# Shared experts woven into the two ends of a state-space layer whose mixing becomes one pipeline over 16 tiles

## The chip, the core and the metric

The kernel runs on one core of one Trainium2 chip. A core has five engines that run at the same time, each through a queue of its own and in the order of that queue: PE (TensorE, matmuls and transposes), DVE (VectorE), ACT (ScalarE), POOL (GpSimd) and SP (SyncE, which here only issues transfers). They meet through semaphores. Transfers between the off-chip memory and the on-chip memory (SBUF) run on 16 DMA engines. Matmul results go to eight banks of accumulation memory (PSUM). The metric is device time in microseconds (us) for one execution, and the time before is the median of three runs.

## The reference, cut to what matters

Input `x` has 8 sequences of 256 tokens, 256 wide, all fp32. Four layers follow one another, each with a residual and a layer norm (no learned scale):

```python
x = _layernorm(x + _L0_attn_ref(x, ...))   # 16 heads of 128, causal
x = _layernorm(x + _L0_ffn_ref(x, ...))    # mixture: 32 experts of width 96, top 6
x = _layernorm(x + _L1_attn_ref(x, ...))   # state-space layer
x = _layernorm(x + _L1_ffn_ref(x, ...))    # mixture: 16 experts of width 176, top 4
```

The first mixture scores the 32 experts by a sigmoid, keeps six a token with weights normed to sum 1, and adds a shared expert of width 192 that every token takes. The second scores 16 experts by a softmax, keeps the best two of four groups of experts, then the best four experts in them, and has a shared expert of width 352. An expert is `(silu(x Wg) * (x Wu)) Wd`.

The state-space layer, for each sequence:

```python
gate, hBC, dt = split(x @ in_proj_w.T)              # 512, 640, 8
h, Bm, Cm = split(silu(causal_conv4(hBC) + conv_b)) # 512, 64, 64
dt = softplus(dt + dt_bias);  A_d = -exp(A_log) * dt
L  = exp(segment_sum(A_d))                          # decay from token s to token l
y  = ((Cm @ Bm.T) * L) @ (h * dt) + carried state + D * h    # 8 heads of 64
yf = y * silu(gate)
return (norm_w * yf * rsqrt(mean(yf * yf) + 1e-6)) @ out_proj_w.T
```

The reference cuts a sequence into chunks of 32 and carries a state between them. The kernel uses chunks of 128, which gives the same sums.

## The kernel before, in words

**Tokens.** The 2048 tokens are four groups (`NG`) of 512, and a group is four tiles (`GT`) of 128. `x` stays in SBUF (`xg[g]`) through all layers.

**Order of the work.** The program is written with generators: a part of the work is a Python generator that yields between steps, and `weave` takes steps from several in turn, each at its own rate. `extras` holds generators from which `extra()` takes a step inside another loop. The result is a program order. A scheduler then orders the instructions of each engine from it by dependences and its own estimates, so an instruction can stand well ahead of its place in the text. At run time each engine takes its own list strictly in order, and a waiting instruction holds up all behind it.

**Mixtures.** `route` (L258 on) makes the choice of experts for one group: turns `x` (L267, L270), logits (L275), top weights (`combine0` or `combine1`), and a row number in the expert's bucket for each choice. For each of the group's four tiles it then fills a buffer `xe` with one row per choice: `x` (L328, ACT), the row's destination (L332, DVE) and its weight (L335, DVE). POOL sends the rows to the buckets in off-chip memory by indirect DMA (L337, one for each choice and tile: 24 a group in the first mixture, 16 in the second). `xe` and the gathered results `gy` share one pool of four buffers (`rowpool`, tag "r").

`sure_tiles` and `other_tiles` make a table of tiles of 128 rows with an expert each: 127 in the first mixture (41 of them known before the last group is routed), 79 in the second (33). `routed` (L530 on) walks the table: load the rows (L558, SP), transpose (L462), gate and up products (L473), SiLU (L478), product (L480), transpose (L489, L491), down product (L500), scale by the weight (L584), and an indirect DMA of the results (L585, POOL). `results` (L599) gathers a token's rows again, `combined` (L622 on) adds them to `x`, and `normed` (L606 on) is the layer norm; its `pow` runs on POOL (L617).

`shared` (L506 on) does one group of the shared expert and calls `extra()` between its steps. `mixture` (L900 on) loads the experts' weights in four parts (two DMAs each, from `load_weights`, L436 on), does `early` groups of the shared expert, the routed tiles, and then `late`. In the first mixture `early` is 3 and the fourth group follows the routed tiles. In the second it is 2 and the other two follow.

**State-space layer.** For each group, `combined` first finishes the first mixture (`all_combined`). `front(g)` then turns `x` (L1034), makes the time steps (`time_steps`, L991 to L1022), the decays `e` for each tile and half of the heads (ACT writes `r` for eight heads, L1067; PE sums, L1071; ACT takes the exp, L956), the convolution (`convolved`: product `cv` L971, first tap on ACT L977, three more on DVE L980), `gm` = C by B (L1099, L1103) and the gates `gt` (L1123). `back(g)` is a pipeline of slots over the group's four tiles: slot s starts tile s (h by dt L1147, `e` by `gm` L1157, state L1165), does y of tile s-1 (L1188, L1196, L1200 to L1209, mean square L1214 to L1216 with a `pow` on POOL), turns tile s-2 (L1225, L1227), and does the output product and norm of tile s-3 (L1235, L1239). So a group has 4 + 3 slots, and the next group's begin after them. `curve` keeps ACT's exps together and its SiLUs together, since they use different tables.

While `back(g)` runs, `weave` mixes in `front(g+1)`, `all_combined(g+2)` and the second mixture's `route(g-1)`; `route(3)` runs beside the second mixture's shared expert and routed tiles. The second mixture's expert weights lie in memory that the state-space layer used, so their load starts when that layer's last step is done.

## Time and profile before

| | us |
|---|---|
| median of three runs (1575.38 to 1586.15) | 1578.88 |
| the profiled execution | 1570.75 |
| its span on the core | 1569.0 |
| PE busy | 1441.7 (92%) |
| DVE busy | 850.4 (54%) |
| ACT busy | 613.9 (39%) |
| POOL busy | 415.8 (27%) |

| stretch of the span, us | what is in it |
|---|---|
| 0 to 688.8 | attention, with the first mixture's routing of groups 0 to 2 |
| 688.8 to 744.7 | start of the first mixture: route(3), shared experts, first rows |
| 744.7 to 930.8 | its 127 routed tiles |
| 930.8 to 1010 | last shared group, the first results gathered, the first front |
| 1010 to 1247 | state-space mixing, up to its last output product |
| 1247 to 1311.1 | start of the second mixture: two shared groups, weights loaded |
| 1311.1 to 1510 | its 79 routed tiles |
| 1510 to 1569 | two shared groups, results, last norms and output |

Durations come from one profiled execution. A line of the profile names the source line, the engine, the operation, what it writes and reads, and how often. "Idle before" is time in which the engine stood before such an instruction, and the name after the arrow is what came last of the things it waited for.

### The profile page before, as it was taken

How to read it: one execution, taken by the hardware profiler on the slowest of the kernel's cores; microseconds unless marked ns; L12 is line 12 of the kernel's file. 1: busy time of each engine (PE TensorE's matmuls, PEld its weight loads, DVE VectorE, ACT ScalarE, POOL GpSimd, SP SyncE). 2: the span in 40 equal slices, each digit the busy share in tenths (PEclk: the TensorE clock that was granted, in tenths of full speed). 3: DMA queues.
4: the chain of work that ended last, by engine and by line, in shares of the span. 5: the costliest groups of instructions: out<-in, count | busy, mean ns of one | idle time of the engine just before them, and what ended most of it. 6: DMA issues, size and time to landing. Idle time of an engine off the chain costs nothing. (4 is left out here: it accounts for less than half of the span.)

```text
span 1569.0 us, 22431 instructions
## 1 busy us (share of the span) xinstructions
PE 1441.7 (92%) x6643; PEld 1025.4 (65%) x6643; DVE 850.4 (54%) x3142; ACT 613.9 (39%) x1620; POOL 415.8 (27%) x474
## 2 busy tenths in 40 slices
PE   8999999999999999987999992899898779999996
PEld 5666666666667666665988881367474647777764
DVE  3444565446445644555655657747565535444457
ACT  3333433334333423341444542675656321333322
POOL 1000014000500032005566661001414315334332
PEclk9999999999999999998999995999999979999998
DMA  9999999900200011058455527100101282332335
GB/s 363 414 413 413 413 408 374 312 4 1 82 1 0 1 44 37 1 166 246 133 181 155 171 85 273 64 1 1 55 1 55 72 251 78 108 106 89 97 116 168
DMA packets 83477, 233.44 MB, mean 149 GB/s; under 512 B 12498, under 2 KB 47345, under 8 KB 81471
## 3 DMA queue, kind: packets, MB, share of 16 engines
q1 hardware_dynamic: 65727, 189.81, 34.7%
q0 software_dynamic: 17632, 42.20, 7.6%
q8 instruction: 56, 0.92, 0.3%
q14 instruction: 62, 0.51, 0.1%
HBM read 80.21 MB, written 157.76 MB: 152 GB/s over the span
## 5 line engine op out<-in xcount | busy, mean ns | idle before, releaser
L769 PE MATMUL qkp<-xT,wattn 128*128 128x512 f32 x512 | 242.0, 594 | 0.0
L804 ACT ACTIVATE pr<-neg,least 128x128 f32<-128x128 f32 (+1 forms) x256 | 114.4, 448 | 296.7 <-DVE least L799 296.6
L337 POOL DMA_INDIRECT m0xs<-m0xe,m0rows x96 | 92.9, 968 | 211.7 <-issue 128.3
L585 POOL DMA_INDIRECT m0ys<-m0ys,m0xl x127 | 125.0, 984 | 67.0 <-ACT m0ys L584 55.8
L777 DVE COPY qk<-qkp 128x512 f32<-128x512 f32 x64 | 44.2, 691 | 171.9 <-PE qkp L769 171.9
L769 PEld LDWEIGHTS qkp<-xT,wattn 128*128 128x128 f32 x512 | 91.1, 191 | 70.0 <-issue 68.5
L754 PE MATMUL vp<-wattn,xT 128*128 128x512 f32 x256 | 117.4, 596 | 4.6 <-ACT xT L218 3.1
L229 POOL TENSOR_TENSOR rstd<-rstd,root 128x1 f32<-128x1 f32 x16 | 8.8, 552 | 424.4 <-DVE rstd L228 422.7
L835 PE MATMUL op<-wattn,z 128*128 128x256 f32 x512 | 120.5, 382 | 0.0
L799 DVE CUSTOM_DVE_ANT_0 neg<-sc,cmask 128x128 f32<-128x128 f32 (+1 forms) x256 | 81.5, 355 | 58.0 <-PE sc L789 57.1
L585 POOL DMA_INDIRECT m1ys<-m1ys,m1xl x79 | 77.7, 984 | 111.4 <-ACT m1ys L584 104.4
L835 PEld LDWEIGHTS op<-wattn,z 128*128 128x128 f32 x512 | 92.6, 190 | 15.0 <-ACT z L857 4.8
L822 PE MATMUL zp<-pT,v 128*128 128x256 f32 x256 | 77.5, 384 | 5.0 <-DVE pT L820 4.9
L337 POOL DMA_INDIRECT m1xs<-m1xe,m1rows x64 | 62.8, 981 | 68.5 <-ACT m1s_1s L478 39.9
L754 PEld LDWEIGHTS vp<-wattn,xT 128*128 128x128 f32 x256 | 46.7, 191 | 48.4 <-issue 40.7
L789 PE MATMUL sc<-qk,qk 128*128 128x256 f32 x256 | 76.5, 380 | 0.0
L810 DVE TENSOR_SCALAR pr<-pr,total 128x128 f32<-128x128 f32 (+1 forms) x256 | 70.1, 318 | 3.3
L822 PEld LDWEIGHTS zp<-pT,v 128*128 128x128 f32 x256 | 47.7, 191 | 36.0 <-ACT z L857 11.8
L617 POOL TENSOR_TENSOR rstd<-rstd,root 128x1 f32<-128x1 f32 x48 | 32.9, 687 | 143.5 <-DVE rstd L616 132.2
L816 PEld LDWEIGHTS pt<-ident,pr 128*128 128x128 f32 x384 | 47.4, 142 | 32.4 <-issue 29.5
L820 DVE COPY pT<-pt 128x384 f32<-128x384 f32 x128 | 67.0, 550 | 2.9 <-PE pt L816 2.1
L785 PEld LDWEIGHTS sc<-qk,qk 128*128 128x128 f32 x256 | 43.7, 190 | 22.7 <-issue 20.4
(2974 smaller groups left out, 3148.6 us busy)
## 6 DMA issues: line engine op xcount, KB each, us to landing
m0xs<-blank SPq DMA_DIRECT2D x9, 7740.0 KB
m1xs<-blank SPq DMA_DIRECT2D x4, 7740.0 KB
m0xl<-m0xs SPq DMA_DIRECT2D x127, 129.0 KB
m0gy<-m0ys SPq DMA_DIRECT2D x16, 768.0 KB
m1xl<-m1xs SPq DMA_DIRECT2D x79, 129.0 KB
m1gy<-m1ys SPq DMA_DIRECT2D x16, 512.0 KB
wattn<-in_w_heads SPq DMA_DIRECT2D x16, 384.0 KB
m0w<-in_w_gu SPq DMA_DIRECT2D x4, 1536.0 KB
```

Source lines behind the costliest of these rows:

```text
L337: ins = nc.gpsimd.indirect_dma_start(out=d["xs"], out_offset=bass.IndirectOffsetOnAxis(ap=rows[:, k, t : t + 1], axis=0), in_=xe[:, k, :], ...
L585: ins = nc.gpsimd.indirect_dma_start(out=d["ys"], out_offset=bass.IndirectOffsetOnAxis(ap=row[:, DM : DM + 1].bitcast(I32), axis=0), in_=y ...
L754: nc.tensor.matmul(ps, lhsT=xT[:, k, t * P : (t + 1) * P], rhs=w_vq[q][:, k, :], start=(k == 0), stop=(k == KC - 1),)
L769: nc.tensor.matmul(ps, lhsT=w_head[h][:, at : at + P], rhs=xT[:, k, :], start=(k == 0), stop=(k == KC - 1),)
L789: nc.tensor.matmul(sc[:, P:], lhsT=qT[:, c0 + P : c0 + SEQ], rhs=kT[:, c0 : c0 + SEQ], start=True, stop=True,)
L799: nc.vector.tensor_tensor_reduce(out=neg[:, cols], in0=sc[:, cols], in1=cmask[:, cols], scale=-SCALE, scalar=3.0e38, op0=ALU.add, op1=ALU.min,
L804: nc.scalar.activation(pr[:, cols], neg[:, cols], AF.Exp, bias=least[:, i : i + 1], scale=-1.0, accum_out=total[:, i : i + 1],)
L810: nc.vector.tensor_scalar_mul(pr[:, cols], pr[:, cols], total[:, i : i + 1])
L816: nc.tensor.transpose(pt[:, i * P : (i + 1) * P], pr[:, i * P : (i + 1) * P], ident)
L820: nc.vector.tensor_copy(pT, pt)
L822: nc.tensor.matmul(zps[:, b * SEQ : (b + 1) * SEQ], lhsT=vs[2 * b][:, cols], rhs=pT[:, : 2 * P], start=True, stop=False,)
L835: nc.tensor.matmul(ps[:, :DM], lhsT=zs[i][:, t * P : (t + 1) * P], rhs=w_head[q * QH + i][:, 4 * P :], start=(i == 0), stop=(i == QH - 1),)
```

## The change

The arithmetic is the same apart from where one product is made. What moves, and where to:

- `shared` becomes a generator, so that it can be woven. In the first mixture only group 0 is done ahead of the routed tiles. Groups 1 and 2 follow after `all_combined(0)`, and group 3 is woven with `front(0)` and `all_combined(1)`. In the second mixture group 0 is woven into the last slots of the state-space layer, group 1 stands ahead of the routed tiles, and groups 2 and 3 follow them as before. The woven ones use a pool of their own (`shsb`, three buffers).
- The expert weights come in eight parts (16 DMAs) for four (8 DMAs). The second shared expert's weights are loaded after the first group's front.
- `back` runs over all 16 tiles as one pipeline of 16 + 3 slots. `front(g+1)` has slots 4g to 4g+4, `all_combined(g+2)` 4g to 4g+3, and `route(g)` 4g+8 to 4g+11, while group g's own tiles start in slots 4g to 4g+3.
- `front` is split into `turned_group`, `decays` (time steps and `e`) and `inner` (convolution, `gm`, gates). For group 0 `inner` comes first.
- `r` for heads 4 to 7 is one DVE product of 128x512 for each tile, in place of four ACT copies of 128x128.
- `e` has 10 buffers for 12, `gt` 7 for 8. The exp in `combine1` is kept with the other exps while the state-space layer runs.

```diff
@@ shared
-                extra()
+                yield
@@ mixture
-            w = load_weights(m, gu, dn, wpool, 0, m.n, 4, f"{m.name}w")
-            for g in range(early):
-                ex.shared(g, wsh)
+            w = load_weights(m, gu, dn, wpool, 0, m.n, 8, f"{m.name}w")
+            for _ in ex.shared(early, wsh):
+                extra()
@@ after0 and the first mixture
-        for g in range(NG - 1, NG):
-            ex.shared(g, wsh0)
-    mixture(M0, w_gu0, w_dn0, wsh0, NG - 1, after0)
-    wsh1 = load_weights(M1, w_gu1, w_dn1, wshared, E1, E1 + 2, 1, "m1ws")
+    mixture(M0, w_gu0, w_dn0, wsh0, 0, after0)
@@ weave
+        for n, gen, start, end in parts:
+            step = (Fraction(end) - Fraction(start)) / (n + 1)
+            live.append([Fraction(start) + step, step, gen])
@@ decays
-                    for i in range(HB):
-                        h = q * HB + i
-                        nc.scalar.activation(
-                            r[:, i, :], tri[:, :P], AF.Copy, scale=a[:, t, h : h + 1]
+                    if q:
+                        nc.vector.tensor_mul(
+                            r, tri[:, :P].unsqueeze(1).broadcast_to([P, HB, P]),
+                            a[:, t, q * HB :].unsqueeze(2).broadcast_to([P, HB, P]),
                         )
+                    else:
+                        for i in range(HB):
+                            nc.scalar.activation(
+                                r[:, i, :], tri[:, :P], AF.Copy, scale=a[:, t, i : i + 1]
+                            )
...
-                    e = act.tile([P, HB, P], F32, name=f"e{g}_{t}_{q}", tag="e", bufs=12)
+                    e = act.tile([P, HB, P], F32, name=f"e{g}_{t}_{q}", tag="e", bufs=10)
@@ front
+            yield from turned_group(g)
+            if g == 0:
+                yield from inner(g)
+                yield from decays(g)
+            else:
+                yield from decays(g)
+                yield from inner(g)
@@ back
-        def back(g):
-            for s in range(GT + 3):
-                t = s
-                if t < GT:
+        def back(lo, hi):
+            for s in range(lo, hi):
+                if s < NG * GT:
+                    g, t = divmod(s, GT)
@@ the order
-        take((COMBINE, all_combined(0)))
-        take((FRONT, front(0)), (COMBINE, all_combined(1)))
-        for g in range(NG):
-            parts = [(BACK, back(g))]
-            if g + 1 < NG:
-                parts.append((FRONT, front(g + 1)))
-            if g + 2 < NG:
-                parts.append((COMBINE, all_combined(g + 2)))
-            if g > 0:
-                parts.append((ROUTE, route(M1, g - 1, w_gate1, combine1)))
-            take(*parts)
+        weave((COMBINE, all_combined(0), 0, 1))
+        for g in (1, 2):
+            weave((SHARED, sh0.shared(g, wsh0), 0, 1))
+        weave(
+            (FRONT, front(0), 0, 1), (COMBINE, all_combined(1), 0, 1),
+            (SHARED, sh0.shared(3, wsh0), 0, 1),
+        )
+        wsh1 = load_weights(M1, w_gu1, w_dn1, wshared, E1, E1 + 2, 1, "m1ws")
+        parts = [(9, back(s, s + 1), s, s + 1) for s in range(NG * GT + 3)]
+        for g in range(NG - 1):
+            at = g * GT
+            parts.append((FRONT, front(g + 1), at, at + GT))
             if g + 2 < NG:
+                parts.append((COMBINE, all_combined(g + 2), at, at + GT - 1))
+            parts.append((ROUTE, routed_group(g), at + 2 * GT, at + 3 * GT - 1))
+        parts.append((SHARED, sh1.shared(0, wsh1), NG * GT, NG * GT + 3))
+        weave(*parts)
@@ after1 and the second mixture
-        ex.shared(NG - 2, wsh1, lambda: finish(2))
-        ex.shared(NG - 1, wsh1, lambda: finish(1))
+        for g, n in ((NG - 2, 2), (NG - 1, 1)):
+            for _ in ex.shared(g, wsh1, lambda: finish(n)):
+                pass
-    mixture(M1, w_gu1, w_dn1, wsh1, NG - 2, after1)
+    mixture(M1, w_gu1, w_dn1, wsh1, 1, after1)
```

## The prediction

> **What bounds the kernel now.** I read the stages first: the span was cut where PE's work changes hands, and each stretch was set against its granted clock and its DMA share. Attention (0 to 688.8 us) is not touched. In this view the first two columns are the stretch and its length, and each engine has its busy us and its instructions.
>
> ```profile
> core 0: us, PE busy (x) PEld busy (x) DVE busy (x) ACT busy (x) POOL busy (x), PEclk, DMA share, GB/s
> 688.80:744.70 55.90, 39.46 (x200) 33.38 (x199) 31.91 (x141) 16.32 (x38) 23.46 (x26) 0.88 0.88 265
> 744.70:930.80 186.10, 183.51 (x1146) 164.68 (x1147) 110.56 (x381) 91.13 (x252) 120.67 (x123) 0.99 0.51 151
> 942.90:1012.00 69.10, 34.62 (x92) 17.54 (x93) 51.58 (x146) 30.79 (x67) 6.90 (x10) 0.68 0.51 183
> 1010.00:1247.00 237.00, 217.55 (x1050) 148.38 (x1049) 142.95 (x527) 136.18 (x299) 57.48 (x70) 0.94 0.06 21
> 1247.00:1264.40 17.40, 5.43 (x8) 2.35 (x8) 4.62 (x29) 4.70 (x8) 13.82 (x17) 0.62 0.96 315
> 1264.40:1311.10 46.70, 42.45 (x182) 30.63 (x183) 21.60 (x107) 12.04 (x27) 5.73 (x6) 0.89 0.52 157
> 1311.10:1510.00 198.90, 197.70 (x954) 146.46 (x953) 88.99 (x258) 62.08 (x157) 85.02 (x88) 1.00 0.31 94
> ```
>
> The reader should see that PE fills both routed stages (744.7 and 1311.1 onward) and most of the state-space stage (1010 to 1247), so PE work added there costs its full time. PE is half idle at four seams: the start of the first mixture, the first front (942.9 to 1012, where DVE is the busy engine and the clock is 0.68), two stalls inside 1010 to 1247, and the tail 1247 to 1311. The change moves PE work between these. Next I read the instructions in time order at each seam; the brackets give the idle time before a row and what ended it.
>
> ```profile
> 731.76 0.48 PE L462 MATMUL m00xp<-ident,m0xl 128*128 128x128 f32 x1 [5.87 <-DMA m0xl<-m0xs]
> ...
> 1119.96 0.17 DVE L332 COPY m1xe<-m1dest 128x4 int32<-128x4 int32 x1 [4.52 <-DMA m1xs<-m1xe,m1rows]
> ...
> 1124.06 3.75 PE L971 MATMUL cv<-xT,win 128*128 128x512 f32 x4 [6.63 <-DVE conv L980]
> 1194.93 3.75 PE L971 MATMUL cv<-xT,win 128*128 128x512 f32 x4 [6.14 <-DVE conv L980]
> ...
> 1246.91 0.33 SPq L444 DMA_DIRECT2D m1w<-in_w_gu  x1
> 1251.05 2.72 PE L473 MATMUL m1s_0gu<-m1ws,m1xT 128*128 128x352 f32 x4 [4.20 <-DVE x L1239]
> 1260.69 2.71 PE L473 MATMUL m1s_1gu<-m1ws,m1xT 128*128 128x352 f32 x4 [6.92 <-DVE x L1239]
> 1313.08 1.42 PE L473 MATMUL m10gu<-m1w,m10xT 128*128 x4 [1.20 <-DVE m11xT L466]
> ```
>
> The first row is the earliest routed tile reaching PE. The next three are one chain: the four `xe` buffers are free only when the scatters that read them have landed, the DVE copy into such a buffer (L332) stands at the head of DVE's queue, the convolution step behind it (L980) is late, and PE's `cv` matmul starves. The last four are the tail: the second mixture's weights are asked for at 1246.9, when the last `out` ends.
>
> **The change, part by part.** Times are against the profiled execution: 1570.75 us, of which the span is 1569.0. The median of the runs shown is 1578.88, so 8.1 us (0.5%) are added at the end.
>
> *Start of the first mixture.* Groups 1 and 2 of its shared expert leave PE. A tile of it is two gate/up sets of 0.65 us (705.28 to 705.93), two transposes of 0.11 and two down sets of 0.43: 2.4 us, 9.5 a group. But 19 us are not won. The weights (4 x 1536 + 4 x 768 KB, issued 689.1 to 694.2) keep the DMA share at 1.01 from 690 to 726, and the first `m0xl` row set, queued behind them, lands for 731.76. Today PE still has shared work up to 744.7; afterwards it waits idle, and the first routed gate/up can follow the transposes and copies by about 4 us: 735.7 for 744.7. **-9** (0 if the tile table or scatters are later than the rows; -12 if the rows come 3 us sooner without the other traffic). POOL has 24 scatters of 0.96 + 0.30 us up to 745.5, and the first result scatters now queue into them; POOL needs 1.28 us a tile to PE's 1.47 (186.1/127), so it catches up.
>
> Eight parts for four means 8 more DMA issues. Row: the eight issues now take 0.33 to 1.7 us each on SP and the engines stay full, so parts overlap and cost 0. The Trainium skill (DMA: Bandwidth & Descriptors, "Anatomy of one DMA") speaks against small parts: each DMA has about 2 us that don't shrink with its size; put end to end that would be +16. The full DMA share decides for 0, and the first row set waits for all parts anyway, so no gain either.
>
> *First front.* Those two groups return here: 19 us of PE at full clock, perhaps 26 at 0.68, inside 34 us of idle PE: hidden. On DVE they aren't: products 2 x 0.24, copies 2 x 0.28, one add 0.42, so 1.5 us a tile and 11.7 for two groups; the r operation adds 4 x 0.68. That makes 51.6 + 11.7 + 2.7 = 66 of 69.1 us. About 5 of this can go into the 12 us in which DVE waits for the first gathered rows (930.8 to 942.9), and before there were 17 us of stalls, of which some 10 remain. Convolution ahead of the time steps for group 0 lets PE start `cv` earlier, but then the decays come last. I take **+2**, with -8 (the order hides all stalls) and +8 (no DVE work goes into the wait) as bounds.
>
> *r by DVE.* 64 ACT copies leave (0.39 us mean, 25 us of ACT) and 16 DVE products of 128x512 come. Nearest row:
>
> ```profile
> L1157 DVE TENSOR_TENSOR e<-e,gm 128x512 f32<-128x512 f32 x32 | 21.2, 677 | 0.0
> L337 POOL DMA_INDIRECT m1xs<-m1xe,m1rows x57 | 56.0, 983 | 66.4 <-ACT m1s_1s L478 39.9 <-issue 12.2 <-DVE m1xe L335 8.2
> ```
>
> So 16 x 0.68 = 11 us of DVE, hidden while DVE is at 60% in the steady stage; were it on the path, +11. ACT's relief is worth at most the 7 us that PE waits for `r`. Here too the skill warns (SBUF — State Buffer, "SBUF: two separate sides"): a DVE operation with two SBUF inputs shuts out a GpSimd operation that reads SBUF for its whole length. By the rule 16 scatters could each wait 0.68, 11 us of POOL. The rows show scatters at 0.983 us in this stage, with many such products beside them, and 0.968 in the first mixture: 15 ns each. I take **0**.
>
> *Steady pipeline.* No boundary is left between `back` calls, but PE is at 29.6 of 30 and 49.0 of 50 us in the stretches between the stalls, so I give that 0. The second mixture's shared expert of group 0 enters slots 16 to 19: per tile two gate/up sets of 1.19, two of transposes 0.22, two down sets 0.87, so 4.55 and 18.2 a group. About 13 of it stands ahead of the last `out` in the changed order, where PE has 2.8 us idle of 47: **+13** (+9 if it fills these and the wait for the last mean square, +16 if DVE's part, 8 us, delays the chain). `e` with 10 buffers for 12 and `gt` with 7 for 8 cost 0 while DVE runs ahead; exp kept beside the other exps saves table loads of 1.28 us on ACT, which is under 60% busy.
>
> The stalls now: PE lost 12.8 us in them (the 6.63 and 6.14 of the two `cv` rows). In the changed order the `xe` copies stand early again, because there are still four buffers and a group's scatters still take 16 x 1.27 = 20 us: group 1's copies wait for group 0's scatters between the convolution steps of the last front, and group 2's wait for group 1's between the gating products (`yf`) of the last `back` tiles. The first place costs PE about 8 us, as each of today's does at 6 to 7; the second about 13, because `rms` and `rstd` on POOL also queue behind the scatters there and no front is left for PE to do meanwhile. That is 20 to 21 for 12.8: **+7** (-5 if the copies pass in time; +27 if DVE stands through both drains, 40.6 us).
>
> *Tail.* From last `out` (1246.9) to `m10gu` (1313.1) are 66.2 us. Two shared groups are done in it, one is left (18.2). In the changed order POOL has the last `rms` ahead of route(2)'s scatters, so the waits of 4.20 and 6.92 shrink. What then ends last is the weights: 8 parts, 8.65 MB, asked for at the last `out`. DMA is at 0.96 till 1264 and falls after about 1280; with the row tiles behind them the floor is near +41. DVE's copies for group 2 and one shared group bring me to +46: **-20** (-25 at the floor, -10 if DVE is held by a whole drain).
>
> Both routed stages and the end (1510 to 1569) keep their instructions: 0.
>
> Sum: -9 + 2 + 0 + 13 + 7 - 20 = **-7 us**: 1563.8 for 1570.75, and 1572 for the median of 1578.9, which is 0.4% less.
>
> **Rivals.**
>
> *Faster, 1548.* A group's route has its slots later, when less of a front is left to hold up: stalls -5 for +7, shared work fills the last drain (+9), the tail reaches its weights (-25), start -10, front 0: -31. For it: 12.8 us of stall and 92 us of idle PE at the seams are there to be filled. Against: the `xe` buffers aren't changed, and they are what stalls.
>
> *Slower, 1602.* DVE's queue stands behind L332 through the whole of each group's scatters: +27 in the steady stage, and in the tail the third drain holds `x` and the shared hidden states (-10 for -20): -9 + 2 + 13 + 27 - 10 = +23. For it: DVE already waits up to 4.8 us in one such copy, and the change adds DVE work ahead of them. It decides once PE loses more than 27 us behind L332 in the steady stage (12.8 + 7 + 7); below that the sum is not above zero. Against: the order puts some `conv` steps and products between one copy and the next.
>
> *The start doesn't move, 1581.* Should the weights, then rows, table and scatters end when the shared work ended, the -9 is gone, and the rest sums to +2.
>
> **How the numbers follow.** Likeliest case 0.42 (its own range 1562 to 1588), faster 0.31, slower 0.21, no start 0.06. One per cent, 16 us, is about what a measurement of this kernel can tell from no change. The likeliest and the no-start case lie within it but for small ends: same 0.43; faster over 1% 0.32; slower over 1% 0.25. The range 1546 to 1601 leaves out a tenth on each side: the faster case's better half-tail, and a stall beyond both drains.
>
> **What would show it.** Start: PE idle from about 712 to 732 and the first `m00gu` near 736. Front: the first `e` by `gm` product near 1003 (1012 less 9), DVE over 85% busy in it. Steady: PE idle of 20 us behind DVE at two places, with L332 behind scatters in DVE's waits. Tail: first `m1w` issue to `m10gu` 46 us. I am wrong if these two places vanish, if the waits at L332 pass 40 us before the last `out`, or if the first front grows beyond 80 us because the shared work runs ahead of the gathers it hides.

## The result, and the profile after

The changed kernel takes 1599.87 us (median of four runs, 1598.53 to 1602.71) for 1582.04 before (1575.38 to 1586.15): a ratio of 1.0119, 95% interval 1.0076 to 1.0162. It is 1.2% slower, where 0.4% less was forecast. The profiled execution took 1601.04 us with a span of 1599.3, against 1570.75 and 1569.0, so the two traces differ by 30.3 us of span. The medians differ by 17.8 only: the profiled execution of the kernel before was 11.3 us faster than this median, so the table adds up to more than the change cost, and which row holds the surplus can't be told. Each stage runs from one event to the next; the marks are read from the two timelines. The first weight issue itself comes 0.7 us later, which with the differences below makes the 30.3 but for rounding.

| from, to | before, us | after, us | difference | forecast |
|---|---|---|---|---|
| first weight issue to first routed gate/up | 55.7 | 41.7 | -14.0 | -9 |
| to the last routed y, and the first gathered rows | 198.2 | 216.8 | +18.6 | 0 |
| to the first `e` by `gm` product (front) | 67.3 | 74.6 | +7.3 | +2 |
| to the end of the last `out` (steady, first part) | 236.7 | 261.2 | +24.5 | +20 |
| to the first issue of the second mixture's weights (steady, the rest) | 0.1 | 14.1 | +14.0 | 0 |
| to the first gate/up of the second mixture (tail) | 66.2 | 42.5 | -23.7 | -20 |
| to the end | 255.9 | 258.7 | +2.8 | 0 |

The view of busy time by stretch, of the changed kernel, with the columns as before:

```profile
689.70:731.40 41.70, 21.07 (x88) 16.88 (x87) 19.42 (x81) 11.95 (x21) 2.77 (x4) 0.66 0.95 273
731.40:760.00 28.60, 18.05 (x87) 15.95 (x87) 10.12 (x39) 4.77 (x15) 21.59 (x24) 0.74 0.37 124
760.00:935.90 175.90, 170.26 (x1059) 152.17 (x1060) 102.41 (x360) 85.66 (x237) 119.92 (x122) 0.99 0.54 158
948.30:1022.90 74.60, 52.23 (x205) 36.31 (x205) 60.05 (x188) 25.44 (x56) 9.30 (x12) 0.80 0.43 152
1022.90:1284.10 261.20, 236.91 (x1111) 160.33 (x1110) 156.43 (x557) 132.67 (x275) 53.59 (x69) 0.91 0.06 22
1284.10:1298.10 14.00, 7.16 (x25) 5.43 (x24) 2.86 (x11) 2.97 (x6) 10.86 (x12) 0.73 0.29 104
1298.10:1340.60 42.50, 27.05 (x117) 19.40 (x116) 18.81 (x107) 8.59 (x17) 3.22 (x4) 0.78 0.89 256
```

The first routed tiles start early and then stall: from 731.4 to 760 PE works only 18 of 28.6 us, while POOL is busy for 21.6. Up to the last `out` there are 19.4 us more of PE work than before, and 24.3 us of PE idle for 19.5. Then comes a stretch of 14 us that the kernel before does not have. In the tail the DMA share is 0.89, for 0.63 before.

Where the early start went is read from the timeline of the changed kernel (POOL, then ACT and PE):

```profile
729.43 1.02 POOL L337 DMA_INDIRECT m0xs<-m0xe,m0rows  x1 [35.92 <-DMA m0xl<-m0xs]
...
752.26 1.00 POOL L585 DMA_INDIRECT m0ys<-m0ys,m0xl  x1 [0.30 <-issue]
...
754.77 0.47 ACT L584 ACTIVATE m0ys<-m04y,m0xl 128x256 f32<-128x256 f32 x1 [9.69 <-DMA m0ys<-m0ys,m0xl]
...
755.30 1.22 PE L500 MATMUL m05y<-m0w,m05hT 96*128 x2 [8.97 <-ACT m0ys L584]
761.68 1.22 PE L500 MATMUL m06y<-m0w,m06hT 96*128 x2 [3.24 <-ACT m0ys L584]
```

The last group's 24 row scatters begin at 729.43, where before they began at 715.33. They waited for a row load (`m0xl`). The first result scatter stands behind 18 of them, at 752.26. There are four `ys` buffers, so tile 4's result waits for a buffer on ACT, and PE stands 9.0 and 3.2 us. Tile 1's `y` is 13.0 us earlier than before, tile 7's 3.1 us later, and from tile 26 on all are 4.9 to 5.0 us later.

What PE waited for from 1022.9 us to the first issue of the second mixture's weights (us in total, times, longest):

```profile
PE m1s_1hp L489 <- DVE m1xe L332: 6.8, 1, 6.8
PE out L1265 <- DVE hd L1176: 5.7, 2, 5.2
PE m1s_1gu L473 <- DVE m1s_0h L480: 4.8, 1, 4.8
PE m1xTp L267 <- ACT x L620: 3.4, 1, 3.4
```

The two `cv` waits of 12.8 us are gone, and these have come. The 14 us are read from the timeline (PE and SP), and from what SP waited for at the first of these issues, in the changed kernel and in the kernel before:

```profile
1250.68 2.72 PE L473 MATMUL m1s_1gu<-m1ws,m1xT 128*128 128x352 f32 x4 [4.85 <-DVE m1s_0h L480]
...
1275.70 1.35 PE L473 MATMUL m1s_0gu<-m1ws,m1xT 128*128 128x352 f32 x4
...
1282.16 1.89 PE L1265 MATMUL out<-wout,yfT 128*128 128x256 f32 x8
...
1294.03 0.63 PE L489 MATMUL m1s_1hp<-ident,m1s_1h 128*88 128x128 f32 x2 [6.84 <-DVE m1xe L332]
...
1296.15 1.91 PE L500 MATMUL m1s_y<-m1ws,m1s_1hT 88*128 88x256 f32 x4
...
1298.13 0.36 SPq L444 DMA_DIRECT2D m1w<-in_w_gu  x1
```

```profile
SPq L444 <- PE m1s_y L500: 264.8, 1, 264.8
```

```profile
SPq L444 <- PE out L1235: 257.2, 1, 257.2
```

The last `out` ends at 1284.05. The second mixture's weights are not asked for then, but at 1298.13, when PE has ended the last down product of the woven shared group. In the kernel before, the same issue waits for the last `out` and follows it by 0.07 us. The reason is read from the kernel: the woven group's pool (`shsb`) is opened together with the state-space layer's pools, and the weights take the memory of that layer when its last step is done, so the group has become one of its steps. Half of the 14 us is one wait of 6.8 us, for a product on DVE that stands behind two others: a copy at L332 that waits 3.5 us for row scatters, and a norm that waits 4.2 us for its power step on POOL, itself behind row scatters.

All eight kernels here with this group in the drain (the last slots of the pipeline) ask for the weights 0.07 us after its last down product, 6.6 to 14.1 us after the last `out`. In the others it is 0.07 us after the last `out`, in one 0.57. No run moved the pool to other memory, so what the 14 us would be worth is not measured.

### The profile page after: what moved, and what is told of

Its sections match the earlier page's. It is cut to its first block, busy times and chain, and to the rows that moved or that the text cites. A ratio compares the mean times of both kernels' runs of the same rounds, so it can differ in the third digit from the quotient of the medians.

```text
span 1599.3 us, 22358 instructions
## 1 busy us (share of the span) xinstructions
PE 1457.3 (91%) x6643; PEld 1037.6 (65%) x6643; DVE 859.8 (54%) x3158; ACT 594.2 (37%) x1556; POOL 414.4 (26%) x474
```

## The experiments

The runs fell on two kinds of chips: on one the kernel before takes 1576 to 1582 us (medians), on the other about 1680, chiefly in attention and the first mixture. Why is left open. So totals are compared as ratios to the kernel before on the same chip, and stages only between chips of one kind. Below, "steady" runs from the first `e` by `gm` product to the first issue of the second mixture's weights, and "tail" from there to the first gate/up. The recorded expectations call that first mark the last `out`, which holds only where the group is out of the drain. "Both back" is the changed kernel with both shared experts where they were.

### The first mixture's shared expert

One part undone: groups 0 to 2 ahead of the routed tiles, group 3 behind them.

```diff
-            for _ in ex.shared(early, wsh):
-                extra()
+            for g in early:                  # first mixture (0, 1, 2), second (1,)
+                for _ in ex.shared(g, wsh):
+                    extra()
...
     def after0(ex):
+        for _ in ex.shared(NG - 1, wsh0):
+            extra()
...
-        for g in (1, 2):
-            weave((SHARED, sh0.shared(g, wsh0), 0, 1))
         weave(
             (FRONT, front(0), 0, 1), (COMBINE, all_combined(1), 0, 1),
-            (SHARED, sh0.shared(3, wsh0), 0, 1),
         )
```

> The changed kernel with the first mixture's shared expert put back where it was: groups 0 to 2 ahead of the routed tiles, group 3 behind them, the rest as changed. Theory (POOL gives the early start back, and the front pays on DVE): the first routed gate/up returns to about 745 us, the last routed y to about 931, the first e by gm product comes 67 us after the first gathered rows instead of 75, so about 12 us less than the changed kernel, near 1588 us. Rival (the early start is worth its 9 to 13 us and the loss lies in the later stages alone): 0 to 9 us more than the changed kernel, 1600 to 1609.

Measured: 1576.38 us, ratio 0.9985 (0.9953 to 1.0017), by the ratios 1.3% (some 21 us) less than the changed kernel and no different from before. The rival falls. The stages, by the same view:

```profile
942.10:1004.30 62.20, 33.39 (x96) 16.97 (x97) 52.34 (x153) 22.57 (x42) 8.81 (x12) 0.70 0.56 203
1004.30:1274.80 270.50, 239.02 (x1123) 162.95 (x1122) 158.39 (x565) 134.88 (x279) 64.82 (x81) 0.91 0.06 22
1274.80:1317.20 42.40, 27.30 (x117) 19.58 (x116) 18.86 (x107) 8.60 (x17) 3.23 (x4) 0.78 0.88 260
```

The first gate/up goes back to 743.89 and the last routed `y` to 929.68, 5.7 us earlier than in the changed kernel. The front takes 62.2 us for 74.6, with 7.7 us less of DVE work. So the three moved groups cost 12.4 us in the front, and the rest of the change makes the front 5.1 us shorter than before. The steady stage is 4.8 us shorter; in the changed kernel some of the last moved group's products had spilled into it.

### The late row scatters

The last group's routing is stepped to its end before the routed tiles are written down; nothing else changes.

```diff
             if m is M0:
                 load_mixer()
+                while len(extras) > 1:
+                    extra()
             ex.routed(w)
```

> The changed kernel with the last group's routing stepped to its end ahead of the first mixture's routed tiles, so that its 24 row scatters no longer wait for the row loads of the first tiles. Theory (POOL's late scatters hold the result scatters): POOL starts them at about 719 instead of 729 us and ends them by 749.5, the y of tile 7 comes at about 755 instead of 765, 9 to 11 us less than the changed kernel, near 1590. Rival (the result scatters are slow for another reason, such as the weights' traffic): no change, 1597 to 1602.

Measured: 1587.52 us, ratio 1.0065 (1.0042 to 1.0089), by the ratios 0.5% (some 8.5 us) less than the changed kernel. The two intervals overlap a little, but the spans of the traces differ by as much, 9.0 us. The timeline:

```profile
720.20 1.02 POOL L337 DMA_INDIRECT m0xs<-m0xe,m0rows  x1 [27.38 <-issue]
...
750.62 1.00 POOL L585 DMA_INDIRECT m0ys<-m0ys,m0xl  x1 [0.30 <-issue]
...
757.11 1.08 PE L500 MATMUL m07y<-m0w,m07hT 96*128 x2
```

The scatters start at 720.2 for 729.4, and tile 7's `y` comes at 757.1 for 764.9: the theory holds. This shows the first half of the loss: `shared` takes an `extra()` step between its own steps, and the routing of the last group lives on those steps. With one group of `shared` for three, there are 10 steps for 30. The scatters then come after the first row loads in the program, and as they write the tensor that those loads read, they wait for them, as the row at 729.43 shows. With that mended, the stretch from the first weight issue to the last routed `y` takes 238.0 us for 241.3 before (245.6 in the changed kernel). So the early start is worth 3.4 us at most: in other traces with the groups ahead, on chips of this kind, the stretch takes 238.3 to 242.5. And 12.4 us are paid for it in the front.

### Four parts

```diff
-            w = load_weights(m, gu, dn, wpool, 0, m.n, 8, f"{m.name}w")
+            w = load_weights(m, gu, dn, wpool, 0, m.n, 4, f"{m.name}w")
```

> The changed kernel with the expert weights in four parts again. Theory: the row scatters of the last group still stand behind the row loads of the first tiles, and those still behind all weights, so 0 to 2 us of difference, 1598 to 1602. Rival (with 16 transfers for eight completion lanes SP cannot send the row loads until 714.7 us, and that delays rows, scatters and results): row loads sent from about 700 us, row scatters from about 720, 8 to 10 us less, near 1591.

Measured: 1600.24 us, ratio 1.0155 (1.0085 to 1.0225), within 0.4 us of the changed kernel's median. With eight parts SP did send the row loads later (714.7 us for 699.2), but they lie behind the weights' data either way. The rival falls, and no cost of eight parts can be told; four runs leave 0.7% on either side.

### The second mixture's shared expert

Group 0 is put back ahead of the routed tiles.

```diff
-        parts.append((SHARED, sh1.shared(0, wsh1), NG * GT, NG * GT + 3))
...
-    mixture(M1, w_gu1, w_dn1, wsh1, 1, after1)
+    mixture(M1, w_gu1, w_dn1, wsh1, (0, 1), after1)
```

> The changed kernel with group 0 of the second mixture's shared expert put back ahead of the routed tiles. Theory (its 29 us of PE in the drain of the pipeline buy 24 us of tail): the steady stage from the first e by gm product to the last out falls from 275 to about 246 us, the tail from last out to the first routed gate/up grows from 42.5 to about 61, in sum 8 to 12 us less than the changed kernel, near 1590. Rival (the order of the pipeline and the later routing cost the time, and the shared work only fills gaps): the steady stage stays at 265 or more and the kernel gets slower, 1605 to 1612.

Measured: 1588.11 us, ratio 1.0073 (1.005 to 1.0097), by the ratios 0.5% (some 7 us) less than the changed kernel; by the spans of the traces 10.1 us.

```profile
1021.70:1263.70 242.00, 219.28 (x1051) 148.95 (x1050) 144.04 (x474) 125.47 (x262) 51.58 (x67) 0.91 0.07 23
1263.70:1333.50 69.80, 52.26 (x202) 37.13 (x202) 33.78 (x203) 16.38 (x34) 23.03 (x25) 0.80 0.60 193
```

The steady stage loses 33.2 us, 14.0 of them the wait of the weights behind the last `out`; the tail gains 27.3, and the end is 3.0 shorter. So the group costs more in the drain than it saves behind it. The rival falls. The theory holds in the main; its tail was expected at 61. The 3 us of the end come with this group: in the traces of this kind of chip the end takes 258.4 to 260.4 us with the group in the drain and 255.7 to 256.0 without. Why is left open.

### What is left with both back

> The changed kernel with both shared experts back ahead of their routed tiles (first mixture: groups 0 to 2 ahead, 3 behind; second: groups 0 and 1 ahead). What is left of the change is the one pipeline, the later routing, the convolution first in group 0, r by DVE and eight weight parts. Theory (the two moves cost separately): 23 and 12 us less than the changed kernel, near 1565 us, with the steady stage near 238 and the tail near 70. Rival (the later routing costs the time whatever lies beside it): the tail and steady stage together stay above 315 us and the kernel stays at the time of before, 1574 to 1580.

Measured, on a chip where the kernel before takes 1681.74: 1677.0, ratio 0.9964 (0.9943 to 0.9985). The theory's 0.99 is missed, but it was taken from times of different chips: by the ratios, the two gains off 1.0119 make 0.994. In the profile steady stage and tail take 241.1 and 69.3 us. On a chip of the first kind the same arrangement with larger pools (the base of the last part below) takes 237.1 and 73.6, 311 in sum for 303 in the kernel before, so these two stages gain nothing from the pipeline and its later routing. But the kernel isn't slower than before, so it is not what costs the 1.2%.

Two parts were then undone on top of both back. For one, `r` of heads 4 to 7 went back to ACT; for the other, `decays` went ahead of `inner` for group 0 too.

```diff
-                    if q:
-                        nc.vector.tensor_mul(r, ...)          # 128x512, DVE
-                    else:
-                        for i in range(HB): ...
+                    for i in range(HB):                       # ACT, all eight heads
+                        h = q * HB + i
+                        nc.scalar.activation(
+                            r[:, i, :], tri[:, :P], AF.Copy, scale=a[:, t, h : h + 1]
+                        )
```

> As the kernel with both shared experts back, with r for heads 4 to 7 written by ACT again (64 copies of 128x128) in place of 16 DVE products. Theory (the product lies beside other work): steady stage and front within 3 us of the kernel with both back. Rival (ACT was the one that PE waited for in the decays): the front grows by 3 to 6 us, the steady stage by 2 to 5.

Measured: 1692.21 us, ratio 1.0057 (1.0038 to 1.0076), 0.9% more than both back. The theory that the product is neutral falls: by the two ratios it is worth about 15 us. Front 59.7 for 61.7, steady 254.4 for 241.1, on a chip of the same kind. The rival expected the front to grow and 2 to 5 us in the steady stage, so it does not fit either. The waits of PE for `r` went from 4.9 to 9.2 us only. The largest new one is for the copy of `yf` on ACT, and PE's row shows it:

```profile
1341.48 1.12 PE L1253 MATMUL yfp<-ident,yf 128*128 128x128 f32 x4 [10.89 <-ACT yfT L1255]
```

A profile of one execution can't say how much of this is ACT's longer list and how much is one unlucky wait. The total gives the size; the mechanism stays open.

```diff
-            if g == 0:
+            if False:
                 yield from inner(g)
                 yield from decays(g)
```

> As the kernel with both shared experts back, with the time steps and decays ahead of the convolution for group 0 as for the others. Theory (the convolution first is what shortened the first front from 67.3 to about 62 us): the front grows back to 66 to 68 us, 4 to 6 us more in all. Rival (r by DVE shortened it): the front stays at 61 to 63.

Measured: 1688.22 us, ratio 1.0052 (1.0034 to 1.007). Front 68.0 for 61.7: the convolution first is what shortened it. The steady stage is 4.4 us longer as well, and by the two ratios the whole 0.9%, more than the 4 to 6 us of the theory.

> As the kernel with both shared experts back, with each group's routing one slot earlier in the pipeline (slots 4g+7 to 4g+10), the earliest that its tiles allow. Theory (group 2's row scatters in the drain hold the last norms and DVE's copies in the tail): the scatters come one slot, about 12 us, earlier, the tail shrinks from about 70 to about 60, 8 us less than with both back. Rival (the scatters hold up the last front's convolution instead, as they did before the change): steady stage 6 to 10 us longer and the sum unchanged within 3 us.

```diff
-            parts.append((ROUTE, routed_group(g), at + 2 * GT, at + 3 * GT - 1))
+            parts.append((ROUTE, routed_group(g), at + 2 * GT - 1, at + 3 * GT - 2))
```

Measured: 1687.18 us, ratio 1.0026 (1.0008 to 1.0044). Steady stage 248.1 for 241.1, tail 70.8 for 69.3. The tail does not shrink, so the theory falls. The steady stage grows as the rival said, but the sum is not unchanged: it is 8.5 us longer. Choosing the experts one slot earlier is worse than the slot of the change.

### What holds the drain

The first theory was that copies into the row buffers, placed a group early, stand in DVE's and ACT's queues until the group before has been scattered. In two runs POOL fills the buffers itself.

```diff
-                nc.scalar.copy(
+                (nc.gpsimd.tensor_copy if m is M1 else nc.scalar.copy)(
                     xe[:, part, :DM], ...
-            nc.vector.tensor_copy(
+            (nc.gpsimd if m is M1 else nc.vector).tensor_copy(
                 xe[:, :, DM : DM + 1].bitcast(I32), ...
```

> As the kernel with both shared experts back, but in the second mixture's routing POOL fills the row buffers (copies of x and the destinations; DVE only the weights), so that no copy that waits for the scatters stands in the queues of DVE and ACT. Theory (those waiting copies hold DVE and ACT, 19 and 25 us in the changed kernel): the waits vanish, the steady stage loses 5 to 10 us and the tail 8 to 12, 15 to 20 us less than with both back. Rival (POOL then holds the norms' power steps behind its copies): each of the 16 copies of 128x512 takes POOL 1 to 2 us, the norms wait longer and it is 5 to 15 us slower than with both back.

> As the changed kernel with only the first mixture's shared expert back (1576.4 us), with POOL filling the second mixture's row buffers. Theory (the shared group in the drain is slow because DVE stands before scatters' buffers): the wait of 6.9 us of a shared transpose for a copy into a row buffer and the two waits of 5 to 8 us by the shared hidden states go, steady stage from 270 to about 255, near 1562. Rival (its work is bound by the chain of norms through POOL): no gain, 1574 to 1590.

Measured: 1.0003 (0.9978 to 1.0027), and 1.0036 (1.0017 to 1.0055) with the shared group in the drain; without the edit they were 0.9964 and 0.9985, so both are slower for it. In the first, steady stage and tail take 239.8 and 77.8 us against 241.1 and 69.3. The first run's rival comes closer: a copy of 128x512 takes POOL 0.64 us only, but DVE's waits for the layer norm's power step on POOL grow from 5.3 to 28.1 us. Next the copies stayed on their engines, but late in the queue.

```diff
                 ins = nc.scalar.copy(xe[:, part, :DM], ...)
+                if m is M1:
+                    tc.add_manual_dep(ins.ins, d["exp"].ins.name, NOSYNC, reason="late")
             ins = nc.vector.tensor_copy(xe[:, :, DM : DM + 1].bitcast(I32), ...)
+            if m is M1:
+                tc.add_manual_dep(ins.ins, weighed.ins.name, NOSYNC, reason="late")
```

> As the kernel with both shared experts back, but in the second mixture's routing the copies into the row buffers are kept late in the queues: the destinations on DVE behind the same group's weights (L322), the rows of x on ACT behind the same group's exp. Theory (copies placed a group early stand in DVE's and ACT's queues until the group before has been scattered, and hold up norms, products and the shared hidden states): the waits of the destination copy for scatters go from about 20 us before the last out and 12 behind it to under 5 each, the steady stage loses 3 to 8 us and the tail 8 to 15, a ratio of 0.983 to 0.99 to the kernel before. Rival (those waits lie beside other waits and cost nothing, as with POOL filling the buffers): ratio 0.994 to 1.0.

> As the changed kernel with only the first mixture's shared expert back, with the same late copies; group 0 of the second shared expert stays in the drain of the pipeline. Theory (the drain is slow because DVE and ACT stand at those copies): steady stage from 270 to 255 to 262 us, tail still near 42, ratio 0.985 to 0.993. Rival (the drain is bound by the chain of norms and routing itself, and shared work there costs its time): steady stage 268 or more, ratio 0.998 to 1.003.

Measured: 1.0022 (1.0006 to 1.0038), and 1.0051 (1.003 to 1.0072), again slower than without the edit. Both theories fall, and the rivals come nearer. In the first of the two kernels the waits of DVE and PE from 1100 us to the second mixture's tiles show where the time went:

```profile
DVE off L623 <- POOL rstd L621: 29.2, 10, 13.3
```

```profile
PE out L1272 <- DVE off L623: 13.0, 1, 13.0
```

DVE's copies no longer wait, and now DVE waits for the layer norm's power step on POOL (`rstd`), which stands behind runs of scatters at 1.27 us each. So there are two queues behind the same scatters. The second one is taken away by giving each tile's four scatters a place behind the power step of a norm.

```diff
+            while behind is not None and not behind(t):
+                yield
...
                 unordered(ins, f"{m.name}xs", d["scatters"])
+                if behind is not None:       # the norm of pipeline tile 4g + 7 + t
+                    tc.add_manual_dep(
+                        ins.ins, behind(t).ins.name, NOSYNC, reason="norms first"
+                    )
```

> As the kernel with both shared experts back, but on POOL each tile's four row scatters of the second mixture stand behind the last power step of a norm of the pipeline, one tile of scatters to a slot, instead of 16 in a row. Theory (16 scatters of 1.27 us in a row hold the norms' power steps for up to 20 us, and the drain and tail wait for those): the wait of DVE for the layer norm's power step falls below 12 us, steady stage and tail together fall from 310 to 285 to 298, ratio 0.983 to 0.992. Rival (later scatters only move the wait to the row buffers' copies and to the tail's row loads): ratio 0.996 to 1.003.

> The same with the copies into the row buffers kept late as well, so that neither the norms' power steps nor DVE and ACT stand behind scatters. Theory (late copies alone only moved the wait from the copies to the power steps, so both must go together): ratio 0.978 to 0.988, tail under 60 us. Rival (PE's own work and the clock bound drain and tail): ratio 0.994 or more.

> As the kernel with both shared experts back, with 12 buffers for e and 8 for gt again (the woven experts' pool is not used). Theory (DVE runs ahead, the two smaller pools cost nothing): ratio within 0.002 of 0.9964. Rival (the front of the next group waits for e buffers of tiles still being mixed): steady stage 3 to 8 us shorter, ratio 0.99 to 0.994.

These ran on one chip, where the kernel before takes 1578.96. The last is both back with the larger pools (`e` 12, `gt` 8) and serves as the base: 1571.29, ratio 0.9949 (0.9924 to 0.9974). Its ratio is no different from the 0.9964 with the smaller pools on the other kind of chip, so these cost nothing that can be told. Spread scatters alone: 1571.62, 0.9951 (0.9919 to 0.9983), no gain. Spread scatters and late copies: 1543.13, **0.974** (0.9674 to 0.9806). DVE's waits in steady stage and tail, first of the base, then with the spread alone, then with both:

```profile
DVE m1xe L332 <- DMA m1xs<-m1xe,m1rows: 29.9, 8, 7.5
...
DVE off L619 <- POOL rstd L617: 11.4, 12, 3.6
```

```profile
DVE m1xe L335 <- DMA m1xs<-m1xe,m1rows: 27.0, 9, 5.7
...
DVE off L626 <- POOL rstd L624: 10.1, 11, 3.1
```

```profile
DVE off L630 <- POOL rstd L628: 11.1, 10, 3.4
...
DVE m1xe L337 <- DMA m1xs<-m1xe,m1rows: 4.0, 1, 4.0
```

With only one of the two edits one of these sums stays near 30 us (29.2 for `rstd` with late copies, on the slower kind of chip; 27.0 for the row copies with the spread). With both they are 11.1 and 4.0, and the steady stage, by the view of stretches, goes from 237.1 to 218.4 us with PE busy for 96% of it, the tail from 73.6 to 62.5:

```profile
1007.00:1225.40 218.40, 209.22 (x1039) 143.57 (x1038) 144.53 (x503) 122.76 (x257) 45.65 (x60) 0.96 0.05 16
1225.40:1287.90 62.50, 46.11 (x202) 32.77 (x201) 31.38 (x174) 18.02 (x37) 29.83 (x33) 0.89 0.75 231
```

This version beats both kernels.

> The changed kernel with only the first mixture's shared expert back, with the spread scatters and late copies; group 0 of the second shared expert stays in the drain. Theory: with norms and copies free of the scatters the shared group fills the drain, steady stage 250 to 260 for 274, tail 42 to 46, ratio 0.978 to 0.99. Rival (the group costs its 18 us of PE and more wherever it lies): steady stage 268 or more, ratio 0.998 or more.

Measured on the same chip, with the shared group in the drain: 1558.03, ratio 0.9841 (0.9774 to 0.9908); steady 243.6, tail 45.9. So with free queues the group still costs 25.2 us ahead of the weights' first issue (18.7 ahead of the last `out`, and 6.5 in which the weights wait for its last product) and saves 16.6 behind it. Why it does not save more is seen in the tail:

```profile
PE m10xp L473 <- DMA m1xl<-m1xs: 14.5, 1, 14.5
```

PE stands 14.5 us for the first row tile, which lies behind 8.65 MB of weights. Work taken out of the tail below that floor buys nothing, and the floor counts from the weights' issue, which the group delays.

> The changed kernel as it is, with only the spread scatters and late copies of the second mixture's routing added. Theory (POOL's runs of scatters and the early copies cost the state-space layer some 20 us in whatever order the shared experts lie, and the two moves cost on top): steady stage 275 to about 250, ratio 0.995 to 1.003, still about 23 us behind the same kernel with the first mixture's shared expert back (0.984). Rival (with the queues free the moved shared work fills the gaps): ratio below 0.99.

> The kernel before with the spread scatters (each tile's four behind a norm of the next group) and late copies, and nothing of the change. Theory (the gain needs the one pipeline with its later routing, in which the scatters fall between the norms of other tiles without the last front's convolution behind them): the two cv waits of 12.8 us go, little in the tail, ratio 0.985 to 0.995. Rival (the queues alone are the gain): ratio 0.98 or less.

Measured on a chip of the slower kind (before: 1679.23): the changed kernel with the two edits 0.9927 (0.9905 to 0.995), steady 252.5 and tail 50.4; the kernel before with them 0.9996 (0.9966 to 1.0027), steady 247.3 and tail 60.5. The first came out better than the theory put it, and short of its rival. On this kind of chip the early start of the first mixture pays: from the first weight issue to the last routed `y` it takes 279.3 us, and 286.6 in the kernel before with the same edits. On the other kind it lost 4.3 us. The kernel before gained nothing from the two edits, less than its theory or its rival had expected. There the scatters stand behind the norms of the next group, not of the tiles 4g + 7 + t, so it is not quite the same edit. What the edits need of the rest of the change was not tried.

## Why the prediction was wrong

The time of 1599.87 lies inside the range, at its edge, but on the other side of no change than the likeliest case. The rival at 1602 is near it in size, not in cause: DVE's waits at L332 in the steady stage are 19.2 us, not two whole drains of 40.6.

**Start of the first mixture (-9): failed, the largest miss.** Start and routed tiles together are +4.6 (-14.0 and +18.6), a miss of 13.6. The gate/up came even earlier than forecast, but the routed tiles were taken to keep their length. What failed is "POOL needs 1.28 us a tile to PE's 1.47 (186.1/127), so it catches up". POOL does catch up, but not before four `ys` buffers are full: PE waited 12.2 us for them (9.0 and 3.2). And I took the scatters to start when they do now. I had read that steps of the routing are taken between those of `shared`, and not counted that two thirds of these steps leave with it. The scatters then wait for loads; I looked at the order of the row loads and not at that of these scatters. The run with the routing finished first gives some 8.5 us back by its ratio, and its trace takes 7.6 less for this stretch.

**First front (+2).** It was +7.3: +12.4 for the moved groups and -5.1 for the rest. DVE's 60.1 us of work is what the sum had (66 less 5). The stalls were taken as 10 and were 14.5, and the gain by the convolution first (6.3 us of front, with both back) was taken as nothing.

**Eight parts (0)** were right as far as four runs can tell. The prediction set 2 us per transfer against it, from the Trainium skill (DMA: Bandwidth & Descriptors, "Anatomy of one DMA"). That section gives them for transfers issued by GpSimd, and SyncE issues these. The price of the product for `r` was right too: 16 at 0.687 us, and the scatters in that stage at 0.970, so the rule that the prediction takes from the Trainium skill (SBUF — State Buffer, "SBUF: two separate sides") cost nothing here. But "0" for moving it was mis-sized: with both back, the run with `r` on ACT puts it at about -15 us.

**Steady stage (+13 and +7): nearly right in sum, not in its parts.** It was +24.5 up to the last `out`. PE's work grew by 19.4 us, not 13, and its idle time by 4.8, not 7. Of the 20 us of idle time that were forecast behind L332, one wait of 6.8 is put down to it, and it falls behind the last `out`; so it is in part luck that the idle time came near. By the count of its products about 13 us of the shared group at full clock do stand there (an estimate, with the prediction's prices), so the term that was mis-sized is their clock: it is 0.77 in the mean from 1260 us to 1298.1. The Trainium skill (TensorE: Matmul & The Clock Gate, "HAM oscillation — how this bites in real kernels") says that gaps in PE's work of more than about 3.4 us bring the slower clock back. The trace agrees with it: after the wait of 4.85 us one gate/up set of four takes 2.72 us, and 1.35 where PE had been running.

**Tail (-20): failed.** The prediction counts it from the last `out` to the first gate/up, and so counted it is -9.7 (66.2 to 56.5). What failed is "8 parts, 8.65 MB, asked for at the last `out`". From their first issue the floor was right (+41 forecast, 42.5 found), but the issue comes 14.1 us after the last `out`, because it waits for the last product of the very group that was moved to fill the drain. I had put this wait at nothing.

**Against the mechanism of the stalls:** I named both queues, the early copies and the power steps, and gave the first the price. The runs show that each hides the other: with both back, neither edit alone gains, and both together give 28 us on one chip. Late copies alone ran only on the other kind of chip.

## What to carry to other kernels

When a piece of work is moved, list what else is driven by its steps: here the routing of another group advanced only while the shared expert was written down. List also what waits for the memory it uses: here the next stage's weights could not be asked for until the moved group was done with it, and 14 us went there. When a wait is removed and nothing is gained, read the same engine's waits again, since a second queue may stand behind the same event; judge two such edits together. A place with idle time is worth its idle time, at the clock found there, only if nothing else bounds it, as the weights bound this tail at about 42 us from their issue.

## What was not expected of the hardware

The same program, the kernel before, took 1576 to 1582 us (medians) on some chips and about 1680 on others, some 6% more, and that is more than any edit here changed. In the traces the first mixture's weights are first asked for at about 690 us on the one and at 731 to 737 on the other, so attention holds nearly half of it. One effect changed its sign with the chip: with the first mixture started early, the stretch from its first weight issue to its last routed `y` was 4.3 us longer on one kind and 7.3 shorter on the other (the latter between two kernels that both have the spread scatters).
